# Reloading the adjacency in eight column parts instead of four

## The chip, the cores and the metric

The kernel runs on one core of a Trainium2 chip. Its time is the device time in microseconds (us) of one launch; of several runs the median is given. Five engines work side by side, each through its own list of instructions: TensorE (PE in the profile, with its weight loads as PEld), VectorE (DVE), ScalarE (ACT), GpSimd (POOL) and SyncE (SP). SyncE, ScalarE and GpSimd also issue transfers (DMAs), which 16 DMA engines carry out.

## The reference

The inputs are node features x (4096 x 512) and an adjacency matrix adj (4096 x 4096, float32) in which about one entry in 500 is set, besides the whole diagonal; the set entries are weights between 0.05 and 1. Two layers follow one another:

```python
# layer 0
a = adj + eye;  d = sum(a, axis=1) ** -0.5
out = relu((d[:, None] * a * d[None, :]) @ x @ W.T + b)
x = layernorm(x + out)
# layer 1: 8 heads of width 64
scores = q @ k.T / 8 + 0.01 * eye - 1e16 * (1 - max(adj, eye))
x = layernorm(x + softmax(scores) @ v @ Wo)      # summed over heads
```

In layer 1 a weight below 1 costs its entry a penalty of the order of 1e15, so that for these inputs a row attends to itself alone, and the layer comes down to a product of the row with one combined 512 x 512 matrix, a residual and a layer norm.

## The kernel before

The function `few_edges_below_one` computes the result under the condition just told, and tests in the same pass that the condition holds. If the test fails, a conditional block runs a general version; with these inputs it doesn't. All times below are of the first.

**Tiles.** The 4096 rows are cut into 32 tiles of 128 rows (NT = 32). A tile of the adjacency is 128 x 4096, 2 MB in all and 16 KB in each of 128 partitions. VectorE looks for the set entries of a tile in eight column segments of 512 (SEGS = 8, SW = 512). In each segment one MAX8 (line 755) takes the eight largest values of every row, and one FIND_INDEX8 (line 756) their columns. Some 20 short instructions then sort the finds of a tile (`sorting`), and `match` brings each row's entries into at most nine slots (KH = 9) with a few small products. A row tile is then the sum of nine gathered rows of y, each times a 128 x 128 matrix.

**First stage, 0 to about 207 us.** Every adjacency tile passes through on-chip memory once, for the sums of its rows. Fourteen early tiles stay long enough to be scanned, and the last five (`resident`) stay in their buffers; the other thirteen (`again`) are only summed and let go. Beside that, y = d * (x W^T) is computed for all rows and stored to DRAM.

**Second stage, from about 207 us.** The loop over i (0 to 33) works on one row tile in each of its turns, in nine steps k, in the order early, resident, again. In a turn:

- `gather` (line 1116) issues nine indirect transfers on GpSimd, each of 128 rows of y, up to 16 ahead of their use.
- `build` (lines 1009 to 1022) makes the matrices s_t on ScalarE; `presum` (lines 1134 and 1136) adds up to three gathered rows on ScalarE and VectorE ("total"); `product` (line 1141) runs the nine products on PE.
- `scaled` and `residual` (lines 1190 and 1198, VectorE) make h; PE transposes it, ScalarE copies it out (hT, line 697) and PE multiplies by the combined matrix (line 706). Layer norm runs on ScalarE and VectorE (lines 1206 to 1225).
- `finish` (lines 1231 and 1232) scales the row tile on ScalarE and issues its store on ScalarE's queue. `load_own` (line 1126 for yo, line 550 for x_t) loads, on SyncE, what the row tile two turns later needs.
- `some` moves the scan on by about eight of its 16 steps for a tile, so that a tile is scanned in about two turns.
- `scan_half` (line 718) tests half an adjacency tile on ScalarE for negative values; the second half of that test is the last reader of the tile. When a buffer has come free, the turn ends with `reload()` (line 996 on), which loads the next of the thirteen tiles through `load_a` (line 541 on; the transfer is line 545) on SyncE.

**Buffers.** The pool `big` has five buffers of an adjacency tile; a reload takes the one that was scanned and tested longest ago. Gathered rows have 18 buffers, yo and x_t three each.

**Order.** The order of each engine's list is laid out before launch by a planner that runs the program on a model of the chip, so that an instruction can stand earlier or later on its engine than in the code; some are pinned to the program's order. Waits between engines and for transfers go by semaphores that the framework assigns. A wait holds up everything behind it on its engine; for SyncE that means the transfers behind it, for ScalarE its arithmetic too.

Of the kernel before, what the change touches and what calls it, by code (L numbers as in the profile page):

```python
# [419 lines left out]
def few_edges_below_one(  # L420
# [27 lines left out]
    SEGS, E = 8, 8  # L448
# [92 lines left out]
    def load_a(t, pool=big, name="a_t", parts=1):  # L541
        a_t = pool.tile([P, N], FP, name=name)
        for c in range(parts):
            o = ts(c, N // parts)
            nc.sync.dma_start(a_t[:, o], adj[ts(t, P), o])
        return a_t
# [14 lines left out]
    def load_first(t, parts=1):  # L561
        if t in early or t in resident:
            return load_a(t, parts=2 if t == NT - 1 else parts)
        return load_a(t, pn, "a_n")

    a_tiles = {0: load_first(0, 4)}
# [378 lines left out]
    def steps():  # L945
# [14 lines left out]
        for n, t in enumerate(order):  # L960
            if t not in a_tiles:
                reload()
            after = sort_some(0 if n < 2 or FULL < n < HELD else 1 if n <= FULL else 2)
            long, idx = scan(t, a_tiles[t])
            begun.append(t)
            for j in range(STEPS):
                long[j]()
                for f in after[j]:
                    f()
                if j == STEPS - 1:  # L970
                    picked.append(t)
                    if t in early:
                        nc.vector.tensor_reduce(  # L973
                            deg_all[:, t : t + 1], v_all[:, t, :], AX.X, ALU.add
                        )
                        scaling(t)
                yield
            waiting.append((t, idx))
# [17 lines left out]
    def reload():  # L996

        t = queue.pop(0)
        reloaded.append(t)
        a_tiles[t] = load_a(t, parts=4)  # L1000

    def spread(t, s_t, k, alone=False):

# [289 lines left out]
    def at(step, i, k):  # L1293

        far = {"T": (2, 0), "M": (2, 6), "Q": (3, 1), "V": (3, 4), "F": (3, 8)}
        near = {"T": (1, 5), "M": (1, 8), "Q": (2, 2), "V": (2, 3), "F": (2, 7)}
        next_to_last = {"T": (1, 2), "M": (1, 3), "Q": (1, 7), "V": (1, 8), "F": (2, 0)}
        for table, tiles in (
            (far, range(NT - 5)), (near, (*range(NT - 5, NT - 2), NT - 1)),
            (next_to_last, (NT - 2,)),  # L1300
        ):
            behind, place = table[step]
            if k == place and i - behind in tiles:
                return i - behind
        return None

    for i in range(NT + 2):
# [6 lines left out]
        for k in range(KH):  # L1314
            ends = p == NT - 1
            t = at("T", i, k)
            if t not in (None, NT - 1):
                hTs[t] = evacuate(later[0], "hT", transpose_rows(hs[t]))
            t = at("M", i, k)
# [61 lines left out]
            t = at("Q", i, k)  # L1381
# [3 lines left out]
            t = at("V", i, k)  # L1385
# [4 lines left out]
            t = at("F", i, k)  # L1390
# [9 lines left out]
            if k == KH - 1 and queue and len(reloaded) < free:  # L1400
                reload()
# [41 lines left out]
```

## Time and profile before

| | |
|---|---|
| median of 3 runs | 620.05 us (618.05 to 621.74) |
| the profiled execution | 617.42 us, of which 615.6 us lie between its first and last instruction (the span) |
| granted TensorE clock | 0.949 of full speed, on average |
| busy: VectorE, PE, ScalarE, GpSimd | 552.1, 518.7, 492.6, 350.7 us |
| moved | 217.68 MB, 354 GB/s over the span |
| adjacency parts of 512 KB | 56 transfers, median 11.5 us from issue to landing |
| of these reloads | 52, issued from 232.8 to 434.5 us |

How to read what follows. In the busy table each engine has its busy time, its share of the span and the number of its instructions. The line of 40 digits cuts the span into 40 equal slices of 15.4 us; each digit is the busy share in tenths, 9 for 90% or more. A line of waits reads: engine and line that waited, what released it, the total in us, how often, the longest. A line of the order in time reads: start and length in us, engine, line, operation, what it writes <- what it reads, how many in a row, and in brackets the idle time before it and its releaser. SPq and ACTq are the transfer-issuing side of SyncE and ScalarE. A releaser is inferred from semaphore events: of several, the one that came last by the profile.

### The profile page before, as it was taken

Reading aid. Unit: us, or ns where it says so; the run is one execution under the profiler, and the core shown is the slowest. Engines: PE = TensorE matmul, PEld = TensorE weight load, DVE = VectorE, ACT = ScalarE, POOL = GpSimd, SP = SyncE. Lnnn points to the kernel's source line nnn. Section 1 sums busy time; section 2 is a strip of 40 time slices with the busy share of each in tenths; the row PEclk is TensorE's granted clock in tenths of the full one; section 3 lists DMA queues with packets and bytes.
Section 4 is the critical chain, followed back from the end, with each engine's and each line's share of the span. In section 5 each row is a group of like instructions: output and inputs, shape, how many; then the busy total and the mean of one; then the engine's idle time right before and its main releaser. Section 6 shows DMA issues by size and latency. Waiting matters only on the chain. (4 is left out here: it accounts for less than half of the span.)

```text
span 615.6 us, 7756 instructions
## 1 busy us (share of the span) xinstructions
PE 518.7 (84%) x1567; PEld 238.0 (39%) x1567; DVE 552.1 (90%) x1986; ACT 492.6 (80%) x1080; POOL 350.7 (57%) x460
## 2 busy tenths in 40 slices
PE   1597577898885399999999999999899979989893
PEld 1343233444332344444434433433343434334341
DVE  5699999999999999999999999998799998995441
ACT  0985766786998797999989999797787987997842
POOL 5132232332314277777777777776777777777740
PEclk9797977998999599999999999999899988999998
DMA  8999999999999969999999999999999888888861
GB/s 325 428 418 425 420 429 405 418 419 423 426 430 423 372 176 334 368 394 400 399 399 397 396 399 397 352 391 366 341 317 370 296 261 294 269 272 289 275 188 39
DMA packets 57273, 217.68 MB, mean 354 GB/s; under 512 B 8701, under 2 KB 9981, under 8 KB 52864
## 3 DMA queue, kind: packets, MB, share of 16 engines
q1 hardware_dynamic: 23888, 115.48, 47.2%
q0 software_dynamic: 28192, 92.30, 42.1%
q10 hardware_dynamic: 5136, 9.31, 4.0%
q14 instruction: 43, 0.35, 0.2%
q8 instruction: 14, 0.23, 0.2%
HBM read 200.28 MB, written 16.78 MB: 353 GB/s over the span
## 5 line engine op out<-in xcount | busy, mean ns | idle before, releaser
L1116 POOL DMA_INDIRECT g<-y,cols_all x288 | 283.2, 983 | 99.4 <-issue 42.8
L1141 PE MATMUL acc<-g,s_t 128*128 128x512 f32 x370 | 181.9, 615 | 8.0 <-DMA g<-y,cols_all 7.7
L755 DVE MAX8 v_all<-a_t 128x8 f32<-128x512 f32 x256 | 168.9, 687 | 8.2 <-DMA a_t<-in_adj_dram 8.2
L756 DVE FIND_INDEX8 idx<-v_all,a_t 128x8 uint32<-128x512 f32 x256 | 175.5, 693 | 0.0
L706 PE MATMUL acc<-wT,xT 128*128 128x512 f32 x256 | 123.2, 630 | 9.5 <-ACT xT L697 8.3
L706 PE MATMUL acc<-wvo,hT 128*128 128x512 f32 x256 | 117.3, 599 | 5.0 <-ACT hT L697 4.0
L718 ACT ACTIVATE dump<-a_t 128x2048 uint8<-128x2048 f32 (+1 forms) x50 | 119.2, 2385 | 2.2 <-DMA a_t<-in_adj_dram 2.0
L1141 PEld LDWEIGHTS acc<-g,s_t 128*128 128x128 f32 x370 | 64.1, 191 | 77.8 <-issue 49.2
L706 PEld LDWEIGHTS acc<-wT,xT 128*128 128x128 f32 x256 | 49.5, 202 | 67.9 <-issue 53.6
L706 PEld LDWEIGHTS acc<-wvo,hT 128*128 128x128 f32 x256 | 48.4, 192 | 66.5 <-issue 54.9
L1136 DVE SCALAR_TENSOR_TENSOR total<-g,wr_all,total 128x512 f32<-128x512 f32 x71 | 52.7, 742 | 15.8 <-DMA g<-y,cols_all 10.7
L725 POOL TENSOR_SCALAR deg<-deg_all 128x1 f32<-128x1 f32 x32 | 7.6, 238 | 93.8 <-DVE deg_all L973 59.4
L1009 ACT ACTIVATE sq<-cols,wr_all 128x128 f32<-128x128 f32 x160 | 58.9, 395 | 0.8 <-ACT r_t L1231 0.4
L1013 ACT ACTIVATE s_t<-sq,wr_all 128x128 f32<-128x128 f32 x128 | 58.2, 487 | 0.4 <-ACT hT L697 0.2
L713 ACT ACTIVATE dump<-a_n 128x4096 uint8<-128x4096 f32 x13 | 47.2, 3630 | 0.0
L697 ACT COPY xT<-pt 128x512 f32<-128x512 f32 x32 | 18.6, 590 | 31.9 <-PE pt L692 26.8
L550 POOL DMA_DIRECT2D x_t<-in_x_dram x32 | 18.1, 568 | 38.0 <-PE pt L692 31.5
L697 ACT COPY hT<-pt 128x512 f32<-128x512 f32 x31 | 17.9, 576 | 26.7 <-PE pt L692 25.2
L1190 DVE SCALAR_TENSOR_TENSOR h<-yo,own_all,acc 128x512 f32<-128x512 f32 (+1 forms) x33 | 23.7, 720 | 12.9 <-PE acc L1141 10.5
L1141 PE MATMUL acc<-total,s_t 128*128 128x512 f32 x54 | 29.3, 626 | 4.2 <-DVE total L1136 4.2
L787 DVE MAX8 top<-key 128x8 f32<-128x56 f32 x192 | 32.3, 203 | 0.0
L692 PE MATMUL pt<-ident,x_t 128*128 128x128 f32 x128 | 21.7, 309 | 10.1 <-DVE above L867 2.5
(139 smaller groups left out, 696.0 us busy)
## 6 DMA issues: line engine op xcount, KB each, us to landing
a_t<-in_adj_dram SPq DMA_DIRECT2D x17, 2048.0 KB, 19.8
a_t<-in_adj_dram SPq DMA_DIRECT2D x56, 512.0 KB, 11.5
a_n<-in_adj_dram SPq DMA_DIRECT2D x13, 2048.0 KB
x_t<-in_x_dram POOLq DMA_DIRECT2D x32, 256.0 KB, 12.8
yo<-y SPq DMA_DIRECT2D x32, 256.0 KB, 8.6
x_t<-in_x_dram SPq DMA_DIRECT2D x32, 256.0 KB, 7.1
out_dram<-r_t ACTq DMA_DIRECT2D x31, 256.0 KB, 7.3
y<-y_t POOLq DMA_DIRECT2D x18, 256.0 KB, 15.0
```

What stands on the lines that cost most here:

```text
L697: copy = nc.scalar.copy(dst.rearrange("p c s -> p (c s)"), pt[:, :D])
L706: nc.tensor.matmul(u, srcT[:, dc, :], w[:, dc, :], start=(dc == 0), stop=(dc == ND - 1))
L713: nc.scalar.activation(dump[:, : part.shape[1]], part, AF.Copy, accum_out=dst)
L718: nc.scalar.activation(dump[:, o], a_t[:, o], AF.Relu, scale=-1.0, accum_out=neg_all[:, t, halves[0] : halves[0] + 1],)
L755: long.append(lambda o=o, seg=seg: nc.vector.max(v[:, o], seg))
L756: long.append(lambda o=o, seg=seg: nc.vector.max_index(idx[:, o], v[:, o], seg))
L787: return lambda: nc.vector.max(top[:, f, r * 8 : r * 8 + 8], keyf[:, f])
L1009: nc.scalar.activation(sq, cols1, AF.Square, bias=wr[:, 2, k : k + 1])
L1013: nc.scalar.activation(s_t[:, k, :], away(), AF.Relu, scale=wr[:, 3, k : k + 1], bias=wr[:, 1, k : k + 1],)
L1116: tc.keep_in_program_order(nc.gpsimd.indirect_dma_start(out=slots[j], out_offset=None, in_=y[:, :], in_offset=bass.IndirectOffsetOnAxis(ap ...
L1136: nc.vector.scalar_tensor_tensor(total[i], g, w, total[i], op0=ALU.mult, op1=ALU.add)
L1141: nc.tensor.matmul(zs[i], mats[i][:, m, :], rows, start=False, stop=stop)
```

## The change

A reload now issues its 2 MB as eight transfers of 128 x 512 (256 KB, 2 KB in each partition) instead of four of 128 x 1024 (512 KB, 4 KB in each partition). Each part is then just one segment of the scan. Reloads alone are touched; the first tile still comes in four parts, the last in two, the others in one.

```diff
         t = queue.pop(0)
         reloaded.append(t)
-        a_tiles[t] = load_a(t, parts=4)
+        a_tiles[t] = load_a(t, parts=SEGS)
```

with, unchanged,

```python
    def load_a(t, pool=big, name="a_t", parts=1):
        a_t = pool.tile([P, N], FP, name=name)
        for c in range(parts):
            o = ts(c, N // parts)
            nc.sync.dma_start(a_t[:, o], adj[ts(t, P), o])
        return a_t
```

## The prediction

> **What bounds the kernel now.** I read the page's busy table and its 40 slices first, then the busy time by stretches of 40 us, then who waits for whom on VectorE and on SyncE's queue, then the order of time on SyncE and ScalarE around one reload, and last the trace's semaphore records of each transfer (number, issue, landing).
>
> ```profile
> PE 518.7 (84%) x1567; PEld 238.0 (39%) x1567; DVE 552.1 (90%) x1986; ACT 492.6 (80%) x1080; POOL 350.7 (57%) x460
> DVE  5699999999999999999999999998799998995441
> DMA  8999999999999969999999999999999888888861
> ```
>
> ```profile
> 280.00:320.00 40.00, 39.71 (x122) 17.70 (x121) 39.91 (x154) 37.43 (x104) 30.55 (x32) 1.00 1.03 399
> 320.00:360.00 40.00, 36.32 (x113) 16.04 (x112) 39.91 (x169) 35.97 (x101) 29.66 (x31) 1.00 1.03 398
> 440.00:480.00 40.00, 36.14 (x104) 15.05 (x103) 34.90 (x143) 29.21 (x87) 29.47 (x30) 0.96 0.96 355
> ```
>
> Columns of the stretches: length, then busy time of PE, weight load, DVE, ACT and POOL, granted clock, DMA share, GB/s. VectorE (39.91 of 40) sets the pace from 40 to 360 us and nearly so to 560; the last 50 us are a tail with little VectorE work. From 240 to 400 us the 16 DMA engines have no room either (1.03). So what counts is whether the change opens or closes a gap on VectorE.
>
> ```profile
> DVE v_all L755 <- DMA a_t<-in_adj_dram: 8.2, 4, 5.8
> ```
>
> ```profile
> DVE h L1190 <- PE acc L1141: 9.3, 4, 4.8
> DVE total L1136 <- DMA g<-y,cols_all: 0.9, 2, 0.6
> ```
>
> The first line is of the whole run: four waits of VectorE for adjacency. The other two are of 207 to 560 us, the time in which reloads are issued and scanned: no wait for adjacency is left there. All four lie in the first tiles, which the change does not touch. The scans of reloads trail their loads by 7 us at the first (issued 232.8, scanned from 239.8) and by some 85 us at the last (434 against 520).
>
> ```profile
> SPq L545 <- ACT dump L718: 48.9, 9, 22.3
> SPq L545 <- DMA yo<-y: 8.6, 6, 2.2
> SPq L545 <- DMA x_t<-in_x_dram: 4.8, 3, 1.9
> ```
>
> Waits of SyncE's queue. A reload (L545) waits for the buffer, which ScalarE's test frees; that is expected. That it also waits for the landing of yo and x_t, with which it shares no data, is the line that carries my forecast. The semaphore records explain it: the hardware transfers of SyncE and ScalarE take turns on eight landing semaphores, and each waits until the one about eight places earlier has landed.
>
> ```profile
> 313.72 1.28 SPq L545 DMA_DIRECT2D a_t<-in_adj_dram  x3
> 317.57 0.33 SPq L1126 DMA_DIRECT2D yo<-y  x1
> 318.78 0.33 SPq L550 DMA_DIRECT2D x_t<-in_x_dram  x1
> 321.89 5.22 SPq L545 DMA_DIRECT2D a_t<-in_adj_dram  x2
> ```
>
> ```profile
> 349.38 0.49 ACT L1013 ACTIVATE s_t<-sq,wr_all 128x128 f32<-128x128 f32 x1
> 350.54 0.34 ACTq L1232 DMA_DIRECT2D out_dram<-r_t  x1
> 350.92 0.58 ACT L697 COPY hT<-pt 128x512 f32<-128x512 f32 x1 [1.06 <-PE acc L1141]
> ```
>
> Three parts of a reload go out at 313.72; the fourth only at 321.89, 0.02 us after the transfer eight places earlier had landed (321.88). ScalarE is in the same rotation: its store at 350.54 goes out 0.08 us after the landing it waited for, and ScalarE stood idle for 1.06 us, which the view puts down to PE because it doesn't name that wait. The stores at 327.36, 338.82 and 360.88 went out 0.47, 0.08 and 0.13 us after theirs; the stores up to 314.3 had 2.4 us or more. So ScalarE is at the edge of this limit between 327 and 361 us.
>
> **The change, part by part.** Thirteen tiles are reloaded, so 52 transfers of 512 KB become 104 of 256 KB; bytes, scans and buffers stay.
>
> *Finer waits for VectorE.* Gain 0, since it never waits for a reload. A wait that is already met costs nothing visible: the start of a scan's MAX8 lies 85 ns before the end of the instruction ahead of it with a DMA wait, and 84 ns without.
>
> *Issue on SyncE.* 52 more at 0.33 to 0.47 us each: the last part of a tile goes out 4 x 0.47 = 1.9 us later. What hides it is the lead of 7 to 85 us. Without it, which only the first reload could lack, VectorE would wait for at most those 1.9 us. The next row's yo and x_t, which stand behind the parts on SyncE, are used almost three rows (some 33 us) after issue.
>
> *ScalarE's test of a half tile* spans four parts instead of two: 26 halves with at most two more waits, at 17 to 28 ns (the semaphore instructions of SyncE): 0 to 1.5 us in all, spread out; I take 0.5, off the path.
>
> *Packets.* The trace gives a packet of 4096 bytes 167.5 ns in this stretch and one of 2048 bytes 88.5 ns (x_t and yo). A tile takes 512 x 167.5 / 16 = 5.36 us of all engines now, 1024 x 88.5 / 16 = 5.66 after: +0.30, 3.9 us over 13 tiles. It lies beside VectorE's work, and lengthens the backlog below by some 0.3 us for each reload.
>
> [...]
>
> *The rotation of eight.* This is the term that I count. A row with a reload now issues 4 + 3 = 7 hardware transfers (parts, yo, x_t, store); then it issues 11. Eight in flight were about 8 x 402 KB = 3.2 MB; they become 2.1 MB. With landings at 13 to 17 us, the hardware side moves 3.2 MB / 16 us = 0.20 MB/us, or 1.3 us for 256 KB. In each reload the store comes third, right after two parts, so the transfer eight back is the fifth part of the reload before. From the landings in the trace, with halves taken at the middle: at 314.3 that part lands at 315.6, and ScalarE is held 1.3 us; at 327.4 it lands at 330.7, 3.3 us; at 336.3 the backlog is 3.3 MB, 13 transfers, eight of them issued, so that the next store waits for six landings, until 344.1 against 338.7: 5.4 us. These do not add up, since a hold lets the backlog drain: the largest counts, 5.4 us. Behind the store on ScalarE stand the hT copy, the s_t tiles and "total"; PE waits for the first two, VectorE for the last. VectorE's slack on ScalarE there is 1.2 us (total ends at 304.4 and is read at 305.5). That leaves 4.2 us on VectorE; the stores at 350 and 361, already at the edge, add about 1. Later gaps of VectorE (1.2 at 411, 4.8 at 447.6) may take some of it back; I take off 1. Bounds: 0, if the planned order puts the store where its semaphore is free, and 10 us (1.3 + 3.3 + 5.4) if the holds do add up.
>
> *Sum.* The profiled execution took 617.4 us (span 615.6 and 1.8 around it). 617.4 + 4.2 + 1 - 1 + 0.3 for the packets = 621.9. The median of the three runs is 2.6 above that execution: 624.5, told as 624.
>
> **Rivals.**
> *Hidden anyway.* VectorE's list is unchanged and the loads have a lead of rows; the planner works with the rotation too and may shift the store. For it: the store at 360.88 stands behind an hT copy that usually follows it. Then 0 to +2: 620 to 622. Against it: the three stores at zero margin.
> *Faster, through the gathers.* Gathers (L1116) move in 4096-byte packets on their own queue, next to reload packets of 4096. If queues take turns by packet, halving the reload's packet lets gathers through sooner. The place: 442.89, where PE waits 2.55 us for a gather while the last reload (issued 432.8 to 434.5, last landing 447.8) is in flight, and VectorE then loses 4.75 us; with 1.15 at 430 and 1.0 at 394 that is at most 6.9. Price: 620 - 5 = 615. It decides if gathers around 440 land at least 2.5 us sooner (their median is 7.4) and ScalarE's holds stay below VectorE's 1.2 us of slack. Against it: VectorE has no gap at all from 280 to 390, where most reloads run.
> [...]
> *The order moves.* The program order is planned before launch; new loads may reorder every engine after 232 us, for 4 us either way: 616 to 624.
>
> **How the numbers follow.** Rotation 0.44 (its own range 622 to 630), hidden 0.32, gathers 0.16, other order 0.08, split evenly between faster and slower. A measurement of this kernel can tell about 0.5% (3.1 us) from no change; the edges are 617 and 623. Of the rotation case I give 0.42 beyond 623 and 0.02 within; hidden is within; gathers are faster. So faster 0.20, same 0.34, slower 0.46. The range 615 to 631 leaves out the upper tail of 10 us with packets on top, and the best of the gathers.
>
> **What would show it.** Right: stores L1232 issued at zero margin to a landing, ScalarE idle before the instruction behind them by 2 to 5 us between 314 and 365 us, VectorE's busy time in 320 to 400 down by about 4 us of 80, and landings of reload parts shorter (about 10 us instead of 15). Step by step: 2048-byte packets at 88 ns; no wait of VectorE for adjacency after 207 us; 104 issues. Wrong: VectorE still at 39.9 of 40 to 360 us means hidden; a vanished gap at 447 us means the gathers; rows that shift before 300 us mean another order.

## The result and the profile after

The changed kernel takes 625.07 us (median of six runs, 624.58 to 627.17) beside 620.08 us for the kernel before (six runs, 618.05 to 621.74): a ratio of 1.0084, with a 95% interval of 1.0065 to 1.0104. The forecast was 624 us and slower, so it came out 1 us low. Ratios here and below are taken over undisturbed runs alone, so that one can differ from the quotient of the medians beside it.

The profiled execution took 624.58 us, with a span of 622.7, beside 617.42 and 615.6 before. The two profiles therefore lie 7.1 us apart and the medians 5.0: the profiled execution of before was faster than its median. Times read from the traces below are on the scale of 7.1.

First the busy table, the slices and the packets of the page of after, with the queue of SyncE's transfers (q1):

```profile
PE 522.4 (84%) x1567; PEld 241.8 (39%) x1567; DVE 552.5 (89%) x1986; ACT 492.5 (79%) x1080; POOL 355.3 (57%) x460
DVE  5599999999999999999799899999998998984441
DMA  8999999999999969999999999999999888888850
DMA packets 64761, 217.68 MB, mean 350 GB/s; under 512 B 9533, under 2 KB 10813, under 8 KB 60352
q1 hardware_dynamic: 31376, 115.49, 47.4%
```

The work is the same (VectorE 552.5 us against 552.1). A dent of VectorE has come where there was none, in slices 20 and 23 (296 to 311 and 342 to 358 us), and the one at 416 to 446 us is gone. The stretches of 40 us show the same trade. First the two of before that the prediction doesn't show, then those of after:

```profile
360.00:400.00 40.00, 38.65 (x115) 15.65 (x114) 38.76 (x168) 34.54 (x104) 30.03 (x30) 1.00 1.01 381
400.00:440.00 40.00, 37.74 (x110) 15.81 (x108) 36.95 (x151) 35.44 (x106) 28.82 (x31) 1.00 0.98 359
```

```profile
280.00:320.00 40.00, 34.27 (x93) 14.67 (x93) 35.24 (x143) 32.71 (x88) 29.52 (x31) 0.91 1.04 391
320.00:360.00 40.00, 35.46 (x108) 15.69 (x107) 36.46 (x156) 32.74 (x96) 27.01 (x27) 0.99 1.01 374
360.00:400.00 40.00, 40.00 (x122) 18.26 (x121) 39.68 (x156) 36.89 (x108) 30.56 (x32) 0.97 1.03 380
400.00:440.00 40.00, 39.59 (x119) 17.09 (x118) 38.73 (x164) 34.17 (x105) 30.70 (x31) 1.00 1.01 372
440.00:480.00 40.00, 36.56 (x112) 15.35 (x111) 37.85 (x162) 33.22 (x99) 30.01 (x31) 1.00 1.01 375
```

VectorE (third pair) has 35.24 and 36.46 us where it had 39.91 twice: 8.1 us are lost from 280 to 360 us. From 360 to 480 it has 116.3 us, where it had 38.76 + 36.95 + 34.90 = 110.6: 5.7 us come back.

The lost part is what the forecast described. The order of time on ScalarE, of after, at two of its stores:

```profile
308.67 0.34 ACTq L1232 DMA_DIRECT2D out_dram<-r_t  x1
309.06 0.49 ACT L1013 ACTIVATE s_t<-sq,wr_all 128x128 f32<-128x128 f32 x1 [5.22 <-DMA a_t<-in_adj_dram]
...
349.70 0.34 ACTq L1232 DMA_DIRECT2D out_dram<-r_t  x1
350.08 0.59 ACT L697 COPY hT<-pt 128x512 f32<-128x512 f32 x1 [4.29 <-DMA yo<-y]
```

ScalarE is idle for 5.22 us, then issues a store, then works on. In the semaphore records of the trace the store at 308.67 goes out 0.08 us after the landing of the transfer whose semaphore it takes over, and so do those at 290.88, 322.36, 335.58, 349.70, 429.97 and 452.13. This time the releaser is named: a part of a reload, or yo, with which neither the store nor the s_t tile shares any data. ScalarE's idle times at these seven are 1.89, 5.22, 1.93, 1.03, 4.29, 4.44 and 1.32 us, 20.1 in all. (In before, ScalarE is idle ahead of one store alone, for 0.7 us.) Behind them VectorE stands, in its order of time and, from 207 to 560 us, in its list of waits:

```profile
310.45 0.21 DVE L1217 TENSOR_SCALAR sums<-sums 128x1 f32<-128x1 f32 x1 [3.57 <-ACT dump L1206]
...
351.99 0.75 DVE L1136 SCALAR_TENSOR_TENSOR total<-g,wr_all,total 128x512 f32<-128x512 f32 x1 [2.90 <-ACT total L1134]
```

```profile
DVE total L1136 <- ACT total L1134: 5.2, 5, 2.9
DVE sums L1217 <- ACT dump L1206: 4.4, 4, 3.6
DVE h L1190 <- PE acc L1141: 3.8, 2, 2.7
```

No wait for adjacency is in this list, as before. What came back can be seen in the waits of VectorE from 360 to 480 us. The first line is of before; the two in the second fence are of after:

```profile
DVE h L1190 <- PE acc L1141: 6.9, 3, 4.8
```

```profile
DVE total L1136 <- ACT total L1134: 1.6, 2, 1.0
DVE h L1190 <- PE acc L1141: 1.1, 1, 1.1
```

A VectorE that arrives 8 us late waits 1.1 us for PE where it waited 6.9. The start of each row's `residual` (line 1198) gives the running account: after trails before by 1.5 us at 294 us, 6.2 at 306, 10.3 at 361, 8.5 at 407, and by only 1.9 at 448. At 483 it is 4.0, at 559 it is 6.0, and 6.7 at the end. So the holds cost 8.8 us by 361, and 8.4 of these were given back by 448. The loss at the end is not simply the hold.

**Where the rest comes from.** GpSimd issues the 288 gathers (line 1116) one behind the other from 216 us to the end of its work. Most take 0.95 us, and the next begins 0.30 us later. These 0.30 us are not counted as busy, so that GpSimd without any free time reads as 76% busy (0.95 of 1.25 us; 30.56 of 40 us from 360 to 400). In order of time, of after:

```profile
321.12 0.95 POOL L1116 DMA_INDIRECT g<-y,cols_all  x1 [0.31 <-DVE v_all L755]
322.38 0.94 POOL L1116 DMA_INDIRECT g<-y,cols_all  x1 [0.30 <-issue]
325.86 1.34 POOL L1116 DMA_INDIRECT g<-y,cols_all  x1 [2.53 <-ACT total L1134]
327.50 0.95 POOL L1116 DMA_INDIRECT g<-y,cols_all  x1 [0.30 <-DVE total L1136]
```

The gap of 2.53 us is ScalarE's hold of 322.36: a gather needs the buffer that "total" reads, and "total" stood behind the store. Four gaps of this kind (at 312.0, 325.9, 338.1 and 352.2 us) make a line among GpSimd's waits that before does not have:

```profile
POOL g L1116 <- issue: 39.3, 129, 0.3
POOL g L1116 <- DMA g<-y,cols_all: 15.0, 48, 0.7
POOL g L1116 <- PE acc L1141: 9.1, 30, 0.3
POOL g L1116 <- ACT total L1134: 7.6, 4, 2.7
```

With the gathers numbered in their order, the difference of the two traces divides as follows ("gap" is the time between gathers beyond 0.305 us each):

| gathers | before: us in gathers, gap | after: us in gathers, gap | lag of after at the end of the stretch |
|---|---|---|---|
| first one starts | at 216.3 | at 218.1 | 1.8 |
| 1 to 72 | 70.2, 0.8 | 70.6, 1.3 | 2.7 |
| 73 to 105 | 32.3, 0.4 | 33.2, 5.1 | 8.4 |
| 106 to 144 | 38.8, 1.6 | 39.1, 0.0 | 7.0 |
| 145 to 198 | 53.6, 3.7 | 53.1, 0.4 | 3.1 |
| 199 to 287 | 87.3, 0.0 | 90.6, 0.0 | 6.4 |

The last gather ends 6.4 us later, and what follows it takes 22.8 us against 22.1. In the gaps the holds take the place of before's own waits (6.7 us in all against 6.5). The difference that stays is a later first gather (1.8 us, before any reload is issued) and gathers that last longer (287.6 us against 283.2), most of it after 481 us, where 25 of 89 take over 1 us instead of 13. At that time all reloads have landed. That the change makes these gathers longer is not shown. In the twelve traces of the experiments below, gathers 199 to 287 take 89.5 to 91.0 us, and the three kernels with four parts and the store on SyncE (90.5 to 90.9 us, 22 to 24 of them over 1 us) are not below the four traces of eight parts (89.8 to 91.0, 22 to 25). So the short stretch is the 87.3 us of before's one profiled execution, and the start varies too: the first gather comes at 216.9 to 218.4 us in eleven of the twelve traces, with no order by parts. Some of the 6.4 us, then, may be the difference of two executions, which are 7.1 us apart where the medians are 5.0. What path the 5.0 take to the end of the kernel stays open.

### The profile page after: what moved, and what is told of

Read it like the earlier page. It is cut to its first block, busy times and chain, and to the rows that moved or that the text cites. A ratio compares the mean times of both kernels' runs of the same rounds, so it can differ in the third digit from the quotient of the medians.

```text
span 622.7 us, 7815 instructions
## 1 busy us (share of the span) xinstructions
PE 522.4 (84%) x1567; PEld 241.8 (39%) x1567; DVE 552.5 (89%) x1986; ACT 492.5 (79%) x1080; POOL 355.3 (57%) x460
## 2 busy tenths in 40 slices
DMA packets 64761, 217.68 MB, mean 350 GB/s; under 512 B 9533, under 2 KB 10813, under 8 KB 60352
## 3 DMA queue, kind: packets, MB, share of 16 engines
q1 hardware_dynamic: 31376, 115.49, 47.4%
## 5 line engine op out<-in xcount | busy, mean ns | idle before, releaser
L1116 POOL DMA_INDIRECT g<-y,cols_all x288 | 287.6, 998 | 101.0 <-issue 39.3
L1141 PE MATMUL acc<-g,s_t 128*128 128x512 f32 x370 | 177.9, 609 | 4.0 <-DMA g<-y,cols_all 4.0
L706 PE MATMUL acc<-wvo,hT 128*128 128x512 f32 x256 | 121.2, 615 | 14.2 <-ACT hT L697 13.2
L718 ACT ACTIVATE dump<-a_t 128x2048 uint8<-128x2048 f32 (+1 forms) x50 | 119.2, 2383 | 0.0
L1141 PEld LDWEIGHTS acc<-g,s_t 128*128 128x128 f32 x370 | 65.6, 192 | 68.4 <-issue 57.2
L706 PEld LDWEIGHTS acc<-wT,xT 128*128 128x128 f32 x256 | 50.3, 205 | 67.8 <-issue 53.6
L713 ACT ACTIVATE dump<-a_n 128x4096 uint8<-128x4096 f32 x13 | 47.2, 3628 | 0.0
L787 DVE MAX8 top<-key 128x8 f32<-128x56 f32 x192 | 32.3, 203 | 0.0
L692 PE MATMUL pt<-ident,x_t 128*128 128x128 f32 x128 | 22.8, 320 | 9.0 <-DVE above L867 2.3
```

Of the source, the lines that this page charges most:

```text
L706: nc.tensor.matmul(u, srcT[:, dc, :], w[:, dc, :], start=(dc == 0), stop=(dc == ND - 1))
L713: nc.scalar.activation(dump[:, : part.shape[1]], part, AF.Copy, accum_out=dst)
L718: nc.scalar.activation(dump[:, o], a_t[:, o], AF.Relu, scale=-1.0, accum_out=neg_all[:, t, halves[0] : halves[0] + 1],)
L787: return lambda: nc.vector.max(top[:, f, r * 8 : r * 8 + 8], keyf[:, f])
L1116: tc.keep_in_program_order(nc.gpsimd.indirect_dma_start(out=slots[j], out_offset=None, in_=y[:, :], in_offset=bass.IndirectOffsetOnAxis(ap ...
L1141: nc.tensor.matmul(zs[i], mats[i][:, m, :], rows, start=False, stop=stop)
```

## The experiments

All of the following ran on three chips on which the kernel before takes 703 to 715 us instead of 620; the record doesn't name the chip of the first result, and that it is another one is taken from the times. The granted TensorE clock is 0.88 to 0.92 there instead of 0.94 to 0.95. Up to 207 us these chips do as the first one does; after that VectorE and GpSimd pause where they did not. Two lines of VectorE's order of time there, from the first kernel below, with a cause the trace does not name:

```profile
237.73 0.24 DVE L784 TENSOR_SCALAR rec<-rec,row1n 128x24 f32<-128x24 f32 x1 [2.72 <-remote]
254.49 0.69 DVE L1198 SCALAR_TENSOR_TENSOR h<-h,x_t 128x512 f32<-128x512 f32 x1 [2.22 <-remote]
```

These traces also lack about half of the semaphore records (6222 updates for the changed kernel there, 12341 on the first chip), so that a releaser in them, named or not, is less sure. Their instructions are complete. GpSimd's gaps come to 74 to 113 us there instead of 7, and a row takes 14 to 16 us on average instead of 12, which gives transfers more time to land. What follows is therefore about parts on such a chip; how far it carries to the first one is told with each. Expectations in us of the first chip can only be read as differences or ratios here.

**The store on SyncE, eight parts.** ScalarE then issues none of these stores, and no landing is named among its waits from 216 to 690 us in the third run.

```diff
-        a_tiles[t] = load_a(t, parts=4)
+        a_tiles[t] = load_a(t, parts=SEGS)
...
-            nc.scalar.dma_start(out[rows, :], r_t)
+            nc.sync.dma_start(out[rows, :], r_t)
```

> Eight parts as in the changed kernel, but the stores of finished row tiles are issued by SyncE instead of ScalarE, so that ScalarE is out of the rotation of eight landing semaphores. Rotation theory: ScalarE's holds and VectorE's gaps between 280 and 360 us (4.8 + 3.5 us against full) vanish; time falls from 625 by 3 to 6 us, to 619-622. Order theory (the other order planned for all engines costs the time, whoever issues the store): stays at 624-627. Packet theory (2048-byte packets slow the transfers): stays at 624-627.

> The run with eight parts and stores issued by SyncE once more, since the chip of the first try took 692 to 712 us for the kernel before. Where the kernel before takes about 620: rotation theory 619-622, order theory or packet theory 624-627.

> Eight parts with the stores issued by SyncE, a third time, for a chip on which the kernel before takes about 620 us. Rotation theory: ratio to the kernel before 0.998 to 1.003, no hold of ScalarE and no gap of VectorE over 0.5 us between 280 and 360 us. Order theory: 1.006 to 1.011 with such gaps gone all the same.

> Eight parts, with the stores L1232 issued by SyncE instead of ScalarE, so that ScalarE waits for no landing. The planned order is close to that of the changed kernel. If the holds of ScalarE are the loss: 0.995 to 1.002 of the kernel before. If the loss lies in the planned order or in more transfers: 1.005 to 1.012, as the changed kernel itself. The numbers differ only where the holds occur, which the trace tells: stores at zero margin to a landing in the kernel before between 327 and 361 us.

Measured against the kernel before on the same chip: 708.28 us beside 705.13, 1.0047 (0.9963 to 1.0130); 710.37 beside 703.47, with no interval; 708.14 beside 706.28, 1.0022 (0.9955 to 1.0089); and 709.37 beside 710.22, 0.9796 (0.9651 to 0.9941), this last with five runs spread from 693.95 to 716.0.

**The store on SyncE, four parts.** The second half of the diff alone.

> Four parts as before, with the stores issued by SyncE: the control for the run with eight. Rotation theory: ScalarE was held only about 1.5 us in all with four parts, so 618-621, and the two runs with stores on SyncE come out within 2 us of each other. Order theory: 5 us below the run with eight parts and stores on SyncE.

> The control with four parts and stores issued by SyncE once more. Rotation theory 618-621 and within 2 us of the run with eight parts; order theory 5 us below it.

> Four parts, with the stores on SyncE. The control for the run beside it: if moving the stores is worth something by itself it is 0.985 to 0.997 of the kernel before, as in two runs so far (0.989, 0.994); if moving them only makes the stores wait on SyncE behind reload parts, 0.998 to 1.005. What the parts alone are worth without the holds is the difference between the two runs.

Measured: 702.36 us beside 705.13, 0.9894 (0.9770 to 1.0019); 697.36 beside 703.47, 0.9944 (0.9904 to 0.9985); 700.60 beside 710.22, 0.9801 (0.9700 to 0.9902). Weighted by their intervals, the three come to 0.992 plus or minus 0.004, and the three of eight parts that have an interval to 1.000 plus or minus 0.005 (an estimate of ours, from the intervals above). So eight parts seem to cost 0.8% plus or minus 0.6 over four although ScalarE issues none of these stores. That is a hint and no more: the three ratios of eight parts scatter more widely than their intervals, and the last pair, run beside each other, has 0.9796 and 0.9801. Nor does the second half of the diff stand alone in its effect: moving the store changes the planned order, by at least 321 of VectorE's 1986 instructions with four parts and 346 with eight, and the two kernels differ from each other in at least 145. One of GpSimd's waits in these two kernels, first with four parts (profiled at 696.7 us), then, on another of the chips, with eight (705.7 us):

```profile
POOL g L1116 <- ACT total L1134: 34.1, 8, 7.7
```

```profile
POOL g L1116 <- ACT total L1134: 42.2, 10, 8.4
```

The wait for "total" is there without any held store. That it is longer with eight parts is not shown: over all traces it is 31.0 to 34.1 us with four parts (three traces) and 31.3 to 42.2 with eight (four). The gaps between gathers are 74.7 and 84.3 us in these two; their difference of 9.6 is close to that of the two executions, 9.0, which fits a gather stream that sets the time here too. Over all traces the gaps overlap (74.7 to 84.7 us with four parts, 79.5 to 87.3 with eight).

**The changed kernel once more**, to have it on such a chip.

> The changed kernel beside the two below, as their reference on the same chip. Where the kernel before takes 620: ratio 1.0065 to 1.0104 as measured at first. Where it takes 705 (the chips of the first three calls, with landings that come later): rotation theory 1.012 to 1.03, since later landings lengthen the holds and the run with stores on SyncE came to 1.002 to 1.005; order theory 1.000 to 1.006, like the run with stores on SyncE.

Measured: 719.06 us beside 714.77, 1.0052 (1.0011 to 1.0093), which agrees with the 1.0084 of the first chip within the intervals. The order on VectorE, ScalarE, PE and GpSimd is that of the first chip's trace, to the last instruction. No store is held: from 207 us on ScalarE is idle for 0 us ahead of every one of them, where it was idle for 17.4 us (20.1 with the issue itself) on the first chip, and no recorded landing comes less than 2 us before its store. So on this chip there is a loss, of 0.1 to 0.9%, without the holds. The range expected by the rotation on such a chip (1.012 to 1.03) was missed; that of the order theory was met, but the next kernel loses as much with the order of before.

**Four parts and four tiny loads.** Behind each part of 512 KB goes a load of 512 bytes into four spare columns of the buffer, so that a reload takes as many places in the rotation as in the change, with the parts of before. What the kernel computes stays whole.

```diff
-        a_tiles[t] = load_a(t, parts=4)
+        wide = big.tile([P, N + 4], FP, name="a_t")
+        for c in range(4):
+            o = ts(c, N // 4)
+            nc.sync.dma_start(wide[:, o], adj[ts(t, P), o])
+            nc.sync.dma_start(wide[:, N + c : N + c + 1], x[ts(t, P), c : c + 1])
+        a_tiles[t] = wide[:, :N]
```

> Four parts of 512 KB as before, and behind each a load of 512 bytes (one float for each row) into four spare columns of the buffer, so that each reload takes eight places in the rotation with the bytes and packets of four; all outputs are computed as before. Rotation theory: as the changed kernel or slower (1.005 to 1.02), stores at 0.1 us after a landing and gaps of VectorE behind them. Packet theory, and any theory by bytes: 0.998 to 1.003.

Measured: 716.31 us beside 714.77, 1.0069 (1.0020 to 1.0118). The order of instructions in this kernel's trace is that of before on PE, VectorE, ScalarE and GpSimd, to the last one, and ScalarE is idle for 0 us ahead of every store from 207 us on. So additions to a reload cost what the change costs, as the rotation theory expected in number, but without its sign of stores close behind a landing, and with no new order, no smaller parts, almost no more bytes and no held store.

It isn't shown, though, that the number of transfers is what costs. The plan and the expectation took the packets to be those of before, and they are not: each tiny load moves one float to each of 128 partitions, 128 packets of 4 bytes. The packets of before, then of this kernel:

```profile
DMA packets 57273, 217.68 MB, mean 354 GB/s; under 512 B 8701, under 2 KB 9981, under 8 KB 52864
DMA packets 64761, 217.71 MB, mean 305 GB/s; under 512 B 16189, under 2 KB 17469, under 8 KB 60352
```

These 7488 more are as many as in the changed kernel (64761 too). At 9 ns each in the trace they are 4.2 us of all engines, close to the 4.6 that the change adds (below). Number of transfers, number of packets and the engines' time all grow here as they do in the change, and the run can't tell them apart.

**Four transfers with pieces of 2 KB.** Packets as in the change, number of transfers as before.

```diff
-        a_tiles[t] = load_a(t, parts=4)
+        a_t = big.tile([P, N], FP, name="a_t")
+        dst = a_t.rearrange("p (s g c) -> p g s c", s=2, g=4)
+        src = adj[ts(t, P), :].rearrange("p (s g c) -> p g s c", s=2, g=4)
+        for c in range(4):
+            nc.sync.dma_start(dst[:, c], src[:, c])
+        a_tiles[t] = a_t
```

> Four transfers of 512 KB, each made of two 2 KB pieces per row (segments s and s + 4), so that the packets are those of the changed kernel and the number of transfers that of the kernel before. Rotation theory: 619-622, since only 0.3 us of DMA time per tile is added. Packet theory: 623-627.

Measured: 711.01 us beside 705.13, 1.0108 (1.0017 to 1.0199). The order is that of before but for 5 of 1986 instructions on VectorE. Stores have 2.9 us or more where a landing is recorded, but ScalarE is idle for 1.9 us ahead of one, at 367.57. That smaller packets alone cost something is not shown, for this cut does something more: with s and s + 4 in one transfer, the second segment of a scan needs the second transfer, where before it came with the first. VectorE then waits for the first reload, which it does for no reload in any other of these kernels, but for one wait of 0.6 us in the next. The line of its MAX8 in this kernel (8.3 us of the 15.1 are at the first tiles, as before):

```profile
L755 DVE MAX8 v_all<-a_t 128x8 f32<-128x512 f32 x256 | 169.6, 690 | 16.1 <-DMA a_t<-in_adj_dram 15.1
```

The two added waits (4.0 us at 249.5 and 2.7 at 259.5) are 6.7 us, and the loss by the ratio is 7.6. What the packets cost was not separated from that.

**Eight transfers with pieces of 4 KB.** Two halves of the rows by four column parts.

```diff
-        a_tiles[t] = load_a(t, parts=4)
+        a_t = big.tile([P, N], FP, name="a_t")
+        for c in range(4):
+            o = ts(c, N // 4)
+            for r in range(2):
+                p = ts(r, P // 2)
+                nc.sync.dma_start(a_t[p, o], adj[t * P + r * (P // 2) : t * P + (r + 1) * (P // 2), o])
+        a_tiles[t] = a_t
```

> Eight transfers of 256 KB for each reload, but cut as two row halves by four column quarters, so that each row's piece is 4 KB as before. Rotation theory: the number of transfers in the rotation is that of the changed kernel, so 623-627 and stores at zero margin to a landing between 290 and 350 us. Packet theory: back to 619-622.

Measured: 725.63 us beside 705.13, 1.0241 (1.0124 to 1.0358). Here the holds are back, and large. The order of time on ScalarE at two stores (line 1238 here) 0.08 us behind a landing, and the longest sum among VectorE's waits from 207 us on:

```profile
341.92 0.34 ACTq L1238 DMA_DIRECT2D out_dram<-r_t  x1
342.30 0.49 ACT L1019 ACTIVATE s_t<-sq,wr_all 128x128 f32<-128x128 f32 x1 [8.22 <-DMA a_t<-in_adj_dram]
...
397.19 0.34 ACTq L1238 DMA_DIRECT2D out_dram<-r_t  x1
397.87 0.58 ACT L697 COPY hT<-pt 128x512 f32<-128x512 f32 x1 [13.58 <-DMA yo<-y]
```

```profile
DVE total L1142 <- ACT total L1140: 55.9, 11, 11.6
```

So a held store of ScalarE does reach VectorE on this chip too, where ScalarE is idle for 8.22 and 13.58 us at two of them and VectorE's waits for "total" come to 55.9 us. The 2.4% are not its price alone: this kernel's 16 DMA engines moved only 271 to 278 GB/s from 320 to 440 us, and VectorE's order differs from the changed kernel's in at least 269 of 1986 instructions. It is the order of the next kernel, to the last instruction on each of the four arithmetic engines.

**Two parts.** The other way: 26 transfers instead of 52.

```diff
-        a_tiles[t] = load_a(t, parts=4)
+        a_tiles[t] = load_a(t, parts=2)
```

> Two parts of 1 MB for each reload: five places in the rotation for each row instead of seven. Rotation theory: no store held at all, 0.99 to 1.00. Fine-wait theory (VectorE profits from small parts): 1.005 or more, with waits of VectorE for adjacency after 232 us.

Measured: 723.27 us beside 714.77, 1.0116 (1.0073 to 1.0160). This is a miss: if fewer transfers in the rotation were all that counts, this kernel had to be at least as fast as before. ScalarE is idle for 0 us ahead of every store, and there are fewer packets than before (53529). VectorE's order differs from before's in at least 242 of 1986 instructions here; whether the order or the coarser parts cost the 1.2% was not separated. Since the kernel just above has the same order, up to about half of its 2.4% may be had without any hold.

## Why the prediction was right, and where not

The time and the sign came out, and the mechanism that it was built on is in the trace. The sum behind the number is not, and that the number is right is luck.

- *Finer waits for VectorE, 0.* Right: no wait for adjacency after 207 us.
- *Issue on SyncE and ScalarE's test, hidden.* Right in effect: 104 issues, ScalarE's tests at 119.2 us as before, and ScalarE 0.0 us idle ahead of them.
- *Packets, 3.9 us of all engines.* About right: q1's share is 47.4% of 622.7 us against 47.2% of 615.6, 295.2 us against 290.6, so 4.6 with rounding of 0.3 on each. That they are worth only 0.3 us of the time is not shown: the two kernels that lost 0.5 to 0.7% without a held store have 7488 more packets each, which add 4.2 us or more, and the DMA engines have no room from 240 to 400 us (share 1.01 to 1.03 before, 1.01 to 1.04 after). A reload part issued from 280 to 400 us lands after 10.3 us (median) instead of 14.4, as forecast (10 instead of 15).
- *The rotation of eight, +4.2 on VectorE and +1 at the later stores.* The mechanism was right, the size too small: 8.8 us by 361. Two things went wrong in the working. The first two stores of the stretch, with 4.3 us to spare before, were taken as free, but the holds began at 290.88 and not at 314. And "these do not add up, since a hold lets the backlog drain: the largest counts" failed: five holds in a row each cost something, and their sum came near to the upper bound of 10. By the early start, the sign "VectorE's busy time in 320 to 400 down by about 4 us of 80" came out at 2.5 us, beside 8.1 from 280 to 360.
- *"I take off 1"* for later gaps of VectorE. This step failed most: 8.4 us came back. Before's gaps at 394, 411, 430 and 447.6 us (8.1 in all) were all named in the working, two of them only under the gathers, but credited with 1; of these, none over 0.8 us was left by 448 but one of 1.04, which is a hold itself.
- *The gathers' rival* named the vanished gap at 447 us as its sign. The gap did vanish, but not because gathers landed sooner: from 420 to 460 us they take 6.4 us to land against 6.2 (medians). From 280 to 400 us they do land sooner, after 6.5 us instead of 9.1; that queues take turns by packet is an assumption which no run shows. The sign had two possible causes, and the forecast allowed it only one.
- *"VectorE sets the pace."* Incomplete: GpSimd's gathers have no free time either, and the 57% of the busy table hid it, since 0.30 us behind each of 288 gathers count as idle. By the gathers, the forecast's terms net out to 0.2 us, and the 6.4 come from 1.8 at the start and 4.4 in longer gathers, which no step had and which may not be the change's.
- *The order moves* was put at 0.08 and read as rows that shift before 300 us. Rows shifted by 1.5 there, which the late start explains; but at least 193 of 1986 VectorE instructions did change places, the first at 240 us, while ScalarE's list from 320 to 520 us stayed, and PE's to 530 but for eight products. The statement that VectorE's list is unchanged was wrong. What that is worth on the first chip is open.

So the figure is right within 1 us by luck: two terms, each wrong by 4 to 7 us, stood against each other, and a difference at the end that no term had took the place of what came back. Its sign rests on firmer ground: four tiny loads beside unchanged parts give it too, if on other chips. Open are whether the longer late gathers belong to the change, by what way the added transfers or their packets cost 0.5 to 0.7% where no store is held, and whether eight parts without the holds would lose on a chip where before takes 620 us; no experiment landed on one. A rival that no run here excludes is the engines' time for the added packets, 4.2 to 4.6 us of all engines, which on the first chip have no room from 240 to 400 us (share 1.01 to 1.04).

The version with four parts and the store on SyncE was faster than before in all three tries (0.992 together), though the interval of one reaches 1.0019. It was not run beside the changed kernel, and not measured where before takes 620 us.

## What to carry to other kernels

A transfer that an arithmetic engine issues can stall that engine on the landing of other transfers with which it shares no data, as here, where ScalarE was idle for up to 5.22 us at a store; look at how soon after a landing it goes out (0.08 us here), before you raise the number of transfers in flight. A hold in the middle of a kernel is worth only what later gaps don't give back (8.4 of 8.8 us came back here), so list those gaps and follow the lag row by row up to the end. And judge whether an engine has room by the interval of its instructions, not by its busy share: GpSimd's gathers, most of them 0.95 us long and 1.25 us apart, read as 76% busy. When a run is built to add one thing alone, see on its page whether it did: the four tiny loads added as many packets as the change.

## What the runs showed of the hardware

- An added transfer brought 16 packets under 512 B: 832 more (9533 against 8701) for 52 more transfers. With 6656 for the halved pieces these are the 7488 packets by which the pages differ (64761 against 57273).
- Most gathers of 128 rows held GpSimd for 1.25 us: 0.95 counted as busy and 0.30 that is not.
- The same program took 620 us where it was first measured and 703 to 715 us on the three chips of the experiments, nearly all of the difference after 207 us, with pauses of VectorE of 2 to 12 us whose releaser the trace, with half of its semaphore records, doesn't name.
